# First loads in the order of the first products, and two key tiles for the keys that are formed early for block 3

## The chip, the cores and the metric

The kernel runs on one core of a Trainium2 chip. The metric is device time in microseconds (us) for one execution; lower is better. Times before are from three runs; in addition one execution was recorded by the hardware profiler, and all traced times below come from that one. The engines are TensorE (PE, with its weight loads shown as PEld), VectorE (DVE), ScalarE (ACT), GpSimd (POOL) and SyncE (SP). In this kernel SP does no arithmetic: it issues the DMAs, one after another, in program order.

## The reference

Two sequences (b = 0 and 1) of 256 tokens with 256 features each run through a "Perceiver" of four blocks. Each block has a cross-attention on a context of 4096 rows of 256 features, a self-attention and a feed-forward. Every part is added to its input after a layer norm without weights:

```
x = x + xattn_n(layernorm(x), ctx[, mask]);  x = x + attn_n(layernorm(x));  x = x + ffn_n(layernorm(x))
```

Three parts matter here.

- Block 0, cross-attention: one head, q = x Wq + bq, k = ctx Wk + bk, v = ctx Wv + bv, softmax with a mask on the context rows.
- Block 0, self-attention: normalized again, q and k are exp(-t*t/2) of a projection, out = q (k^T v) / (q sum(k) + 1e-6) over 16 heads; then a scaled norm, a 512-wide product with GELU, and a product back. Block 0, feed-forward: `h = silu(x w1) * (x w2)` (1024 wide), `gelu(h h1)`, `gelu(h h2)`, `h w3`; h1 and h2 are 1024 by 1024.
- Block 3, cross-attention: 16 heads of 16 features on the same context, `k = ctx k_w + k_b`, `v = ctx v_w + v_b`. Its keys and values depend on the context alone, so nothing in blocks 0 to 2 has to be done before them.

## The kernel before

**Arithmetic.** Nearly every product of 32-bit numbers is made of three products: each operand is a pair of tiles, a rounded high part `h` and the rest `l`, and `mm3` issues h·h, h·l and l·h. `split` (L394 to L407) makes the pair from a raw tile: ACT casts the high part (L404, or L401 with a bias), and DVE (L407, or L402 with a bias) or POOL (L406) subtracts for the low part. A weight is loaded raw (tile `wr`, L340), then split into `w`.

**Two lanes.** Tiles of the left lane have names that begin with `a`, those of the right lane with `x` (so `xkvk` is tile `kvk` of lane x, `awr` a raw weight of lane a). Each lane has its own PSUM tags and pools. The program is written lane after lane; a scheduler of the tile framework, which has its own model of the engines, sets the order in which each engine issues the instructions of both lanes. All DMAs are issued by SP in that order. An instruction waits for what it reads, and a write to a tile waits until the readers of its earlier contents are done; with `bufs=1` a tile name has one buffer, with `bufs=2` two that alternate.

**The start.** `run` (L1814 on) loads the unit matrix `eye`, both halves of x (L1818), `cols` (columns of biases and scales, L1820), the constants `first` and `unmask`, computes `w1h` and `w12` from `cols` on DVE (L1827, L1828), and calls `gone_keys` (L1305 to L1307: it loads the key mask, inverts it on DVE and writes it to device memory as `gone_d`; the attention reads it back, L716). Then `x_queries(0, xb[0])` loads x0.wq and x0.wk, normalizes x[0] (`layernorm`: L426, L427 and L432 on DVE, the power on POOL L417, the scaling L441 on DVE), transposes it on PE (L449), splits it (`axnT`) and makes the queries. After it `prep_alone(xp, 0, FIRST)` loads the weights x3.wk and x3.wv and forms the block-3 keys and values of units 0 and 1 of sequence 0.

**Keys and values of block 3.** The context of a sequence has 8 units of 512 rows. For each unit `prep_alone` (L847) loads two raw tiles of the transposed context (L859), splits each (`kx`; ACT high, POOL low) and calls `prep` (L865). `prep` does, for each half m of the features: 12 matmuls into PSUM, then ACT writes the high part and DVE the low part of tile `kvk`, and SP writes both to device memory (L876, `akh_d` and `akl_d` in the trace, 256 KB each). Then POOL sets ones in the value tile `kvv` (L878, one buffer), 24 more matmuls follow, DVE (L384) and ACT (L386) copy two results each into `kvv`, and SP writes it (L886, `av_d`, 544 KB). The same names serve three calls that stand in `run` as

```
FIRST, BEFORE, BEHIND = (0, 2), (2, 4), (4, 6)
...
self.prep_alone(xp, 0, range(*self.BEFORE), 2)
...
xb[1] = self.l0_attn(x, 1, xb[1], w0)
...
xb[0] = self.l0_ffn(0, xb[0], fp)
xq[0] = self.x_queries(1, xb[0])
self.prep_alone(xp, 0, range(*self.BEHIND), 2)
```

FIRST works in the large pool "x" and has two buffers for `kvk`. BEFORE and BEHIND, units 2 to 5, work in a smaller pool "x0", and `prep_alone` passes on `bufs=1 if bufs else 2`: one buffer for `kvk` there. The m = 1 half of a unit can then be written only after the DMAs that read the m = 0 half have landed.

**The stage with units 2 to 5.** Lane a runs `l0_ffn(0, ...)` (L984): w1 and w2 (with a tanh on ACT and `ag`, `au` on DVE), the 16 weight pieces of h1 and h2, each loaded, split and used for 24 matmuls (the GELU is L1010 on ACT), and w3 with its scaling on DVE (L1017) and the sum on POOL (L1018). Lane x runs units 2 and 3, then `l0_attn(1, ...)` (L904), then units 4 and 5. When `l0_ffn` is through, lane a goes on with `x_queries(1, xb[0])`: layer norm, transposes, casts, products. The next stage opens pool "x" again; its first context loads wait until those products are done.

**Pool "x0".** `l0_attn` gets its tiles from the same memory: `xr` and the scaled, transposed `xrTs`, `sq`, `kx`, `vx`, `kv`, `u`. `rmsnorm_t` (L891) takes a tile of the tag `xr`, too; `transposed` (L452) names the scaled tile after its tag, `xrT` + "s".

## Time and profile before

| what | value |
|---|---|
| median of three runs | 1523.76 us (1521.26 to 1531.1) |
| the profiled execution's own time | 1522.72 us |
| its span | 1520.9 us, so 1.82 us lie around it |
| mean granted TensorE clock | 0.942 |
| PE busy | 1354.9 us, 89% of the span |
| DVE, ACT, POOL busy | 1111.6, 890.3, 519.4 us |
| moved by DMA | 212.00 MB, mean 139 GB/s |

The span is the recorded stretch from the first to the last instruction. A row of the trace's timeline reads: start, duration, engine, source line, operation, output tile, input tiles, number, and in brackets the idle time of the engine just before, with what ended it. So `[3.63 <-DMA av_d<-xkvv]` says that the engine stood for 3.63 us until the DMA that reads tile `kvv` had landed. In a table of windows each row is a stretch of the span: its borders, its length, and for each engine the busy time and the number of instructions, then the granted clock, the share of the DMA engines in use and GB/s.

### The profile page before, as it was taken

To read this page: it belongs to the slowest core of one execution; us is meant where nothing else is said; L and a number is where in the kernel's file an instruction comes from. 1 tells how busy PE (TensorE), PEld (TensorE's weight loads), DVE (VectorE), ACT (ScalarE), POOL (GpSimd) and SP (SyncE) were. 2 spreads that over 40 slices of the span, in tenths; PEclk is the share of its full clock that TensorE was granted. 3 is DMA by queue.
4 is the path that set the end of the run, shared out by engine and by line. 5 is a ranking of instruction groups with operands and counts; after the bars stand their busy time and mean duration, and the time that the engine had idled before them with its cause. 6 is when DMAs were issued, how large, how long until landed. Compare 5 with 4: busy or idle time off the path is not lost.

```text
span 1520.9 us, 29330 instructions
## 1 busy us (share of the span) xinstructions
PE 1354.9 (89%) x11278; PEld 1109.5 (73%) x11278; DVE 1111.6 (73%) x1879; ACT 890.3 (59%) x1668; POOL 519.4 (34%) x389
## 2 busy tenths in 40 slices
PE   6998787968999998998998777899999999988698
PEld 6898787968998998998898435555555554874598
DVE  6999854437567878885578598799999961566675
ACT  6676555538776655764663302788888888233243
POOL 6755343236355544664335403000000000531130
PEclk9999999989999999999999859899999999996699
DMA  8754164556465657455632542343333311401262
GB/s 291 245 153 127 42 187 136 175 178 208 150 192 171 178 176 211 147 155 178 182 108 90 186 161 90 112 123 105 123 119 106 116 53 52 144 1 32 82 219 73
DMA packets 125143, 212.00 MB, mean 139 GB/s; under 512 B 12840, under 2 KB 89240, under 8 KB 121480
## 3 DMA queue, kind: packets, MB, share of 16 engines
q1 hardware_dynamic: 125004, 210.13, 44.9%
q8 instruction: 89, 1.46, 0.4%
q14 instruction: 50, 0.41, 0.1%
HBM read 181.32 MB, written 28.61 MB: 138 GB/s over the span
## 4 chain that ended last, share of the span: by engine, by line
PE 40%; DVE 24%; DMA 5%; ACT 4%; POOL 3%; issue 3%; SPq 1%; DVEq 0%; ACTq 0%; POOLq 0%
DVE xpm L1377 14%; PE amm L413 8%; PE xmm L413 6%; PE xacc L581 4%; PE xs L413 4%; PE xpr L413 4%; DMA awr<-in_w 3%; PE xf L1375 2%; PE amm L1398 2%; PE amm L1771 1%; PE xmm L785 1%; POOL aw L406 1%; ACT aw L404 1%; PE amm L581 1%; DVE aw L407 1%
## 5 line engine op out<-in xcount | busy, mean ns | idle before, releaser
L1377 DVE TENSOR_REDUCE xpm<-xf 128x2 f32<-128x1024 f32 x256 | 310.6, 1233 | 10.1 <-PE xf L1375 8.8
L1399 ACT ACTIVATE xp<-amm 128x512 f32<-128x512 f32 x342 | 194.6, 595 | 33.5 <-PE amm L1398 16.7
L406 POOL TENSOR_TENSOR aw<-awr,aw 128x1024 fp32r<-128x1024 f32 (+1 forms) x53 | 126.3, 2384 | 160.2 <-ACT aw L404 128.1
L404 ACT CAST aw<-awr 128x1024 fp32r<-128x1024 f32 (+1 forms) x112 | 114.0, 1020 | 102.7 <-DMA awr<-in_w 53.2
L413 PE MATMUL xmm<-xvx,xpT 128*128 128x256 f32 x1152 | 167.2, 291 | 5.0 <-DVE xpT L788 2.2
L413 PE MATMUL xs<-xkx,xqkT 128*128 128x256 f32 x1152 | 162.0, 285 | 1.5 <-POOL xkx L735 0.7
L735 POOL TENSOR_TENSOR xvx<-xraw,xvx 128x512 fp32r<-128x512 f32 x96 | 132.6, 1397 | 87.4 <-ACT xvx L733 82.9
L581 PE MATMUL xacc<-xp,xv 128*17 128x256 f32 x2048 | 161.0, 387 | 0.9 <-DVE xot L599 0.9
L1375 PE MATMUL xf<-xk,xq 64*128 64x512 f32 x512 | 135.3, 526 | 21.8 <-DVE xpm L1377 14.2
L413 PEld LDWEIGHTS xmm<-xvx,xpT 128*128 128x128 f32 x1152 | 147.9, 193 | 8.4 <-issue 3.7
L413 PEld LDWEIGHTS xs<-xkx,xqkT 128*128 128x128 f32 x1152 | 147.5, 191 | 3.4 <-POOL xkx L735 0.9
L1375 PEld LDWEIGHTS xf<-xk,xq 64*128 64x128 f32 x512 | 51.2, 196 | 126.3 <-issue 79.9
L407 DVE TENSOR_TENSOR aw<-awr,aw 128x1024 fp32r<-128x1024 f32 (+1 forms) x59 | 83.3, 1415 | 64.9 <-ACT aw L404 63.0
L1398 PE MATMUL amm<-xq,xk 64*128 64x256 f32 x684 | 112.4, 294 | 2.7 <-DVE aqT L402 2.6
L1422 POOL TENSOR_TENSOR ax<-ax,ax 128x128 f32<-128x128 f32 x8 | 3.7, 458 | 324.2 <-DVE ax L611 324.2
L1399 ACT ACTIVATE xp<-xs 128x512 f32<-128x512 f32 x170 | 101.2, 595 | 16.5 <-PE amm L1398 11.8
L413 PE MATMUL amm<-ah,aw 128*128 128x256 f32 x768 | 102.2, 290 | 9.3 <-ACT au L1010 4.9
L413 PE MATMUL amm<-axnT,aw 128*128 128x256 f32 x636 | 99.0, 313 | 10.9 <-ACT axnT L404 4.8
L1398 PEld LDWEIGHTS amm<-xq,xk 64*128 64x128 f32 x684 | 95.4, 187 | 17.2 <-issue 12.8
L413 PEld LDWEIGHTS amm<-ah,aw 128*128 128x128 f32 x768 | 96.9, 195 | 12.3 <-ACT au L1010 5.5
L413 PEld LDWEIGHTS amm<-axnT,aw 128*128 128x128 f32 x636 | 90.9, 216 | 18.5 <-ACT axnT L404 6.5
L735 POOL TENSOR_TENSOR xkx<-xraw,xkx 128x512 fp32r<-128x512 f32 x48 | 73.0, 1521 | 85.0 <-ACT xkx L733 84.8
(593 smaller groups left out, 2835.5 us busy)
## 6 DMA issues: line engine op xcount, KB each, us to landing
awr<-in_w SPq DMA_DIRECT2D x105, 512.0 KB
xraw<-in_ctxT SPq DMA_DIRECT2D x108, 256.0 KB
xraw<-in_ctx SPq DMA_DIRECT2D x96, 256.0 KB
xk<-akh_d SPq DMA_DIRECT2D x64, 256.0 KB
av_d<-xkvv SPq DMA_DIRECT2D x16, 544.0 KB
xv<-av_d SPq DMA_DIRECT2D x32, 272.0 KB
akh_d<-xkvk SPq DMA_DIRECT2D x32, 256.0 KB
akl_d<-xkvk SPq DMA_DIRECT2D x32, 256.0 KB
```

Of the source, the lines that this page charges most:

```text
L404: nc.scalar.copy(dst.h, src)
L406: return lo.tensor_tensor(dst.l, src, dst.h.bitcast(F32), ALU.subtract)
L407: return nc.vector.tensor_sub(dst.l, src, dst.h)
L413: tie(self.nc.tensor.matmul(out, lhsT=x, rhs=y, start=start and i == 0, stop=stop and i == 2))
L581: inst = self.nc.tensor.matmul(acc[STRIP * j : STRIP * j + v(j).shape[1], :S], lhsT=v(j), rhs=p[:, j, :], start=start, stop=stop)
L735: nc.gpsimd.tensor_tensor(x.l, r, x.h.bitcast(F32), ALU.subtract)
L785: tie(nc.tensor.transpose(pst[:, t * P : (t + 1) * P], p[:, t * P : (t + 1) * P], self.eye))
L1375: tie(nc.tensor.matmul(both[:, h * 512 : (h + 1) * 512], lhsT=q4[rows, j, t * P : (t + 1) * P], rhs=k4[rows, j, :], start=True, stop=True))
L1377: nc.vector.tensor_reduce(at, both.rearrange("p (h n) -> p h n", h=2), axis=AX.X, op=ALU.max)
L1398: tie(nc.tensor.matmul(ps[h][:, j, :], lhsT=ks[c][rows, a + j, s * P : (s + 1) * P], rhs=q4[rows, a + j, :], start=True, stop=True))
L1399: exps = [nc.scalar.activation(p[:, h, a : a + 2, :], ps[h], AF.Exp, scale=0.25) for h in range(2)]
L1771: nc.tensor.matmul(ps[:, f, :], lhsT=w1[half][:, c, f * P : (f + 1) * P], rhs=buf[:, c, e * cap : (e + 1) * cap], start=c == 0, stop=c == 1)
```

## The change

1. **Start.** Only x[0] is asked for ahead of the first weights. The load of `cols` is given to `x_queries` as `behind` and asked for behind the loads of x0.wq and x0.wk. `gone_keys()`, the load of x[1], the constants `first` and `unmask`, and the DVE computations of `w1h` and `w12` stand behind `prep_alone(xp, 0, FIRST)` in the program.
2. **Keys.** `prep_alone` no longer passes a number of buffers to `prep`, so `kvk` has two buffers in pool "x0" as well. `kvv` keeps one.
3. **Room.** In `l0_attn` the second result of the layer norm takes tag `kv` in place of `xr`, the scaled transposed tiles take tag `kx` in place of `xrTs`, and the tile of `rmsnorm_t` takes tag `u` with two buffers. The tags `kv`, `kx` and `u` belonged to tiles of `l0_attn` that are written later.

No arithmetic is added or removed.

```diff
-    def transposed(self, x, pool, tag, n=2, scale=None, bias=None, plain=None, bufs=1):
+    def transposed(self, x, pool, tag, n=2, scale=None, bias=None, plain=None, bufs=1, scaled=None):
...
-                u = self.t(pool, [P, 2, S], tag + "s", bufs=1)
+                u = self.t(pool, [P, 2, S], scaled or tag + "s", bufs=1)
...
-    def x_queries(self, n, x):
+    def x_queries(self, n, x, behind=lambda: None):
...
         wq, wk = k.weights(f"{pre}.wq", f"{pre}.wk")
+        behind()
...
-            self.prep(xp, b, u, kx, *w3, bufs=1 if bufs else 2)
+            self.prep(xp, b, u, kx, *w3)
...
     def rmsnorm_t(self, k, x, ap, scale):
-        xr = k.t(ap, [P, 2, D], "xr")
+        xr = k.t(ap, [P, 2, D], "u", bufs=2)
...
-        return k.transposed(xr, ap, "xrT", scale=scale)
+        return k.transposed(xr, ap, "xrT", scale=scale, scaled="kx")
...
     def l0_attn(self, k, b, x, wp=None):
-            xn, xr = k.layernorm(x, ap, second=("xr", D / self.RMS**2, 0.0))
+            xn, xr = k.layernorm(x, ap, second=("kv", D / self.RMS**2, 0.0))
...
-            xrT = k.transposed(xr, ap, "xrT", scale="a0.s1")
+            xrT = k.transposed(xr, ap, "xrT", scale="a0.s1", scaled="kx")
...
     def run(self):
-        for b in range(B):
-            nc.sync.dma_start(xb[b], self.ins["x"][b * S : (b + 1) * S, :].rearrange("(t p) d -> p t d", p=P))
+        load_x = lambda b: nc.sync.dma_start(xb[b], self.ins["x"][b * S : (b + 1) * S, :].rearrange("(t p) d -> p t d", p=P))
+        load_x(0)
         self.cols = a.t(self.fix, [P, NCOL], "cols")
-        nc.sync.dma_start(self.cols, self.ins["cols"])
-        self.first = a.const(self.fix, "first")
-        self.unmask = a.const(self.fix, "unmask").to_broadcast([P, S])
+        self.w1h, self.w12 = a.t(self.fix, [P, 8], "w1h"), a.t(self.fix, [P, 8], "w12")
...
-        self.w1h, self.w12 = a.t(self.fix, [P, 8], "w1h"), a.t(self.fix, [P, 8], "w12")
-        nc.vector.tensor_scalar(self.w1h, a.col("f0.w1", 0, 8), 0.5, None, ALU.mult)
-        nc.vector.tensor_mul(self.w12, self.w1h, a.col("f0.w2", 0, 8))
-        self.gone_d = self.gone_keys()
...
-                        xq = {0: self.x_queries(0, xb[0])}
+                        xq = {0: self.x_queries(0, xb[0], lambda: nc.sync.dma_start(self.cols, self.ins["cols"]))}
                         self.prep_alone(xp, 0, range(*self.FIRST))
+                        self.gone_d = self.gone_keys()
+                        load_x(1)
+                        self.first = a.const(self.fix, "first")
+                        self.unmask = a.const(self.fix, "unmask").to_broadcast([P, S])
+                        nc.vector.tensor_scalar(self.w1h, a.col("f0.w1", 0, 8), 0.5, None, ALU.mult)
+                        nc.vector.tensor_mul(self.w12, self.w1h, a.col("f0.w2", 0, 8))
                         xb[0] = self.xattn(xp, 0, 0, xb[0], xq[0])
```

## The prediction

> **What bounds the kernel now.** The page's busy table comes first: PE is busy 89% of the span at a mean granted clock of 0.942, and the chain that ended last is PE 40%, DVE 24%, DMA 5%. So only a stage in which PE stands idle can give time to this change. The table of windows shows three (borders, length, busy time and instructions of PE, PEld, DVE, ACT, POOL; clock; DMA share; GB/s):
>
> ```profile
> 7.70:48.00 40.30, 33.43 (x237) 31.23 (x238) 30.83 (x42) 28.34 (x51) 32.04 (x20) 1.00 0.94 320
> ...
> 187.00:312.70 125.70, 109.05 (x816) 104.91 (x817) 61.16 (x96) 63.90 (x106) 51.26 (x34) 0.95 0.56 170
> 312.70:337.30 24.60, 13.60 (x80) 12.06 (x80) 9.38 (x25) 7.16 (x13) 6.45 (x6) 0.73 0.50 141
> ```
>
> The start is bound by transfers: a DMA share of 0.94. The stage from 187 us, in which units 2, 3 and 4 are formed beside l0_ffn(0) and l0_attn(1), leaves PE idle 125.70 - 109.05 = 16.65 us. The seam, from the end of l0_ffn's last product (312.7, called T0 below) to the next stage's loads, leaves 11.00 us at a clock of 0.73.
>
> Who ends the idle time in the stage is told by its waits (total, times, longest):
>
> ```profile
> ACT aw L404 <- DMA awr<-in_w: 20.8, 11, 3.9
> ...
> PE xpr L413 <- DVE xkvk L402: 6.8, 2, 3.5
> ...
> PE amm L413 <- ACT au L1010: 4.7, 2, 3.9
> ...
> ACT xkvk L401 <- DMA akl_d<-xkvk: 3.7, 2, 3.0
> ```
>
> The last line is the single kvk tile. The first is its competitor: lane a stands for weights.
>
> The timeline shows the waits for both kinds of tile, in the stage and in the seam:
>
> ```profile
> 221.09 0.42 DVE L384 COPY xkvv<-xmm 128x256 f32<-128x256 f32 x1 [3.63 <-DMA av_d<-xkvv]
> ...
> 223.35 1.69 PE L413 MATMUL xpr<-xw,xkx 128*128 128x256 f32 x12 [3.46 <-DVE xkvk L402]
> ...
> 229.36 0.69 ACT L401 ACTIVATE xkvk<-xmm,acols 128x512 fp32r<-128x512 f32 x1 [3.04 <-DMA akl_d<-xkvk]
> ...
> 323.75 0.69 ACT L401 ACTIVATE xkvk<-xmm,acols 128x512 fp32r<-128x512 f32 x1 [4.68 <-DMA akl_d<-xkvk]
> ...
> 325.60 1.22 PE L449 MATMUL amm<-ac_eye,axn 128*128 128x128 f32 x4 [7.45 <-DVE axn L441]
> ```
>
> PE's 3.46 us at 223.35 name kvk, but kvk stood behind the value copies, which waited for av_d (issued at 213.01, landed at 221.09: 8.08 us). That is kvv's single tile, which stays single. At 323.75 it is kvk: akl_d was issued at 316.84 and landed 6.9 us later; DVE stood behind ACT, the layer norm's scaling (325.14) behind DVE, and PE for 7.45 us.
>
> **The start.** Before, the first weight is asked for at 4.26, behind x[1], cols, first, unmask and the key mask, and ACT casts it at 8.37. DVE does x[1]'s statistics (0.72 us and more, from 5.07) ahead of the value that POOL's power waits for. Meanwhile the DMA engines are not full:
>
> ```profile
> 2.00:3.00 1.00, 0.00 (x0) 0.00 (x0) 0.00 (x0) 0.01 (x1) 0.00 (x0) 1.00 0.77 160
> ...
> 5.00:6.00 1.00, 0.00 (x0) 0.00 (x0) 1.00 (x9) 0.00 (x0) 0.00 (x0) 1.00 0.56 52
> ```
>
> From 2 to 7 us the shares are 0.77, 0.98, 0.76, 0.56 and 0.78, so 1.15 us of transfer time is lost. After, SP issues eye, x[0], the lane-a weight, cols, the lane-x weight and four context tiles, then the key mask, x[1], first, unmask. The weight is asked for about 2.6 us earlier. POOL's low part of it (9.49 to 11.85) then follows the power, which starts 0.8 us earlier (x[1]'s statistics are gone): from about 7.2, 2.3 us earlier, and with it the four low parts of the context tiles (6.53 us from 11.81). Against this, DVE's low part of axnT (0.69 at 9.94) now stands behind that of the lane-x weight (2.06), about 1.4 later. From 7 to 24 us DMA runs at 0.9 and more, so what is regained of its time counts most: I take **-1.5**, between 1.15 and 2.3 and nearer the transfers. Ends: -3 (POOL's 2.3 and x[1]'s statistics in full), +1 (the DVE order, and the mask's round trip, now behind the weights and the context, late for the first softmax).
>
> **The stage up to T0.** No instruction is added to the arithmetic. With two tiles both halves of a unit's keys stand together on ACT and DVE, with no DMA between them. The order of the program moves, too: w1 and w2 of l0_ffn come ahead of l0_attn(1)'s exponentials and of unit 3, and the largest part of the new order is at the end: PE issued 34 matmuls of units 4 and 5 behind T0 (10 + 5 + 5 + 2 + 12 on the timeline from 312.52), and now issues 70, so 36 leave the stage. Before T0, 28 matmuls of the w3 product take 3.50 us (309.18), 0.125 each, and 36 take 4.5 us, moved into a seam with 11 us of idle PE. The key tile's stall at 229.36 left PE idle 1.44 at 231.48, which goes. Sum **-5.9**. What is late next is lane a's weight: a pair comes every 7.2 to 8.5 us on the timeline.
>
> Ends: -14.3, if all idle time goes but 3.46 at 223.35 and 3.36 at 189.39, in the end of the attention before (16.65 - 6.82 = 9.8), and the 4.5 come on top; +2.6, if nothing is won and two more ACT table loads (tanh and exponential now alternate; 1.28 us each at 0.73) stand bare. I cost them at nothing because ACT is busy 63.90 of 125.70 us. The tags kv, kx, u cost nothing either: they add one wait, POOL's sum `base` for DVE's low part of xrT, and POOL is busy 51.26 of 125.70.
>
> **The seam.** The stall of 4.68 on ACT goes, but the LN's way does not come free. POOL's memset of unit 5's kvv now stands ahead of the LN's power, and ACT's copies into it ahead of the axnT cast; both wait until unit 4's av_d has landed. On SP that av_d stands behind two weight loads, the second of which waits for a POOL low part: this load was issued at 317.97, T0 + 5.3. From there av_d takes 4.4 (issued 307.93, memset at 312.30) to 8.1 us; then memset 0.22, power 1.37, scaling 1.37, transposes 1.24. So axnT is cast at T0 + 13.9 to 17.6, where it was 326.86 - 312.68 = 14.18: -0.3 to +3.4. I take the middle, **+1.6**. PE does the 70 matmuls in this time, 70 x 0.125 = 8.75 us, so the value tile's wait hides them; without it the 36 would cost their 4.5 again.
>
> A rule weighed against the rows. The rows: akl_d took 6.9 us from issue to landing, av_d 4.4 and 8.1. The Trainium skill (DMA: Bandwidth & Descriptors, Anatomy of one DMA) gives one transfer a fixed part of about 2.0 us, mostly completion latency, and its 256 KB at 436 GB/s another 0.6; by that estimate a second tile could win 2.6 us at most where the rows lose 6.9. The rows decide, since these writes share the engines with weight loads. A second rule speaks for more: after the 7.45 us idle, 12 matmuls took 3.45 us against 1.60 at full clock. The skill (TensorE: Matmul & The Clock Gate, Part 1) puts the drop to half clock after some 3.4 us idle; a seam without such a gap would win those 1.85 us too. I leave them out, since the value tile keeps a gap.
>
> After the seam the program's order is the same but for small swaps: 0.
>
> **The sum**, on the profiled execution's own 1522.72 us (span 1520.9 and 1.82 around): -1.5 - 5.9 + 1.6 = -5.8, so **1516.9**. The median of the runs is 1.04 higher.
>
> **Rivals.**
>
> 1. *The keys held up the whole chain.* For it: 6.8 us of PE waits on kvk, and the chain of waits in the seam runs through 6.81 us of akl_d. Against: 20.8 us of ACT waits for weights. Then all of -14.3 comes, and the seam its -0.3: 1522.72 - 1.5 - 14.3 - 0.3 = 1506.6. Chance 0.13.
> 2. *The single value tile takes the keys' place* (slower). Place: unit 3's value copies on DVE and ACT, ahead of lane a's copies. SP issues unit 2's av_d behind a weight load that waits for a cast and a POOL low part (1.05 + 2.39 = 3.44). If the flight (8.08) and this lie bare, PE stands 11.52, of which 3.46 were there: +8.06, and the seam's end of +3.4: 1522.72 - 1.5 - 5.9 + 8.06 + 3.4 = 1526.8. It decides once the added value waits pass the 7.4 us won at the start and before T0. For it: 7.13 on POOL and 3.63 on DVE at 221.1. Against: av_d also landed in 4.4. Chance 0.2.
> 3. *The change gives no lead:* weights set T0 whatever the keys do. For it: the 20.8 us. Against: PE's waits on kvk. Only the start and the seam count: 1522.72 - 1.5 + 1.6 = 1522.8. Chance 0.22.
>
> **How the numbers follow.** The forecast has 0.45. The ends add up to 1522.72 - 3 - 14.3 - 0.3 = 1505.1 and 1522.72 + 1 + 2.6 + 3.4 = 1529.7; rounded out by the 1.04 between profile and median the range is 1504 to 1531 and takes in all rivals. One per cent, about what a measurement of this kernel can tell from no change, is 15.2 us: faster is below 1508.5, most of rival 1 with a little of the forecast, 0.12; slower is above 1539, only what I have not thought of, 0.05; the rest 0.83.
>
> **What would show it.** Start: first weight cast on ACT near 6, attention's steps some 1.5 earlier at 48 us. Stage: no wait of ACT's kvk for akl_d, T0 near 312.7 - 7.4 = 305.3, stalls of value copies on av_d no longer than 4. Seam: POOL's memset of kvv, not kvk, as the last wait ahead of the LN, some 26 us from T0 to the next stage's first load (now 24.6). I am wrong if a stall on av_d of 8 us or more stands bare on PE, or if l0_ffn's weights come no earlier than before.

## The result, and the profile after

The kernel became slightly **slower**: the median of 22 runs is 1530.33 us (1523.37 to 1535.76), against 1524.65 us (1514.68 to 1534.88) of 22 runs of the kernel before. The ratio is 1.0039, 95% interval 1.0021 to 1.0057, or about 5.7 us more where 5.8 us less were forecast. The recorded execution took 1535.49 us, with a span of 1533.7 us and a mean granted clock of 0.936 (0.942 before); it is among the slowest of the 22.

The table of windows for the kernel after, with the borders moved to about the same places of the program (304.10 is 1.3 us behind T0, which is 302.8 here), and then the stage behind the seam, which the prediction did not show (start:end, length, then busy time and number of instructions of PE, PEld, DVE, ACT and POOL, granted clock, DMA share, GB/s):

```profile
9.45:48.00 38.55, 31.44 (x226) 29.48 (x227) 30.55 (x41) 23.49 (x44) 27.75 (x18) 1.00 0.92 298
187.00:304.10 117.10, 103.60 (x803) 99.65 (x804) 67.93 (x96) 66.77 (x106) 51.01 (x31) 0.99 0.54 175
304.10:324.80 20.70, 15.04 (x107) 13.98 (x106) 9.50 (x26) 7.75 (x17) 8.95 (x8) 0.92 0.60 189
...
324.80:350.00 25.20, 18.59 (x125) 18.19 (x124) 18.71 (x25) 16.58 (x30) 15.59 (x11) 0.82 0.69 219
...
400.00:440.00 40.00, 33.97 (x243) 33.33 (x244) 15.83 (x26) 29.78 (x45) 13.45 (x8) 0.87 0.42 136
440.00:485.00 45.00, 41.60 (x328) 41.25 (x328) 32.71 (x67) 26.31 (x57) 22.29 (x17) 0.92 0.53 161
```

The same view of the kernel before, for that stage:

```profile
337.30:360.00 22.70, 18.95 (x153) 18.37 (x152) 20.34 (x26) 18.73 (x34) 17.61 (x10) 0.99 0.83 247
...
400.00:440.00 40.00, 37.15 (x301) 35.92 (x300) 20.81 (x37) 32.01 (x51) 17.78 (x11) 1.00 0.52 160
440.00:485.00 45.00, 43.94 (x369) 43.48 (x367) 33.85 (x74) 26.79 (x59) 22.89 (x17) 1.00 0.59 179
```

The two stages on which the prediction worked did become shorter: from 187 us to T0 115.8 us for 125.7, and 22.0 for 24.6 from T0 to the last border, with a clock of 0.92 for 0.73 in the seam. The next stage lost it again. In the 40 us from 400 to 440 PE did 243 matmuls, where the kernel before did 301 in the same time, at a clock of 0.87 for 1.00.

The waits of the kernel after in the stage up to the seam (engine, line, releaser: total, times, longest, in us):

```profile
ACT aw L404 <- DMA awr<-in_w: 16.2, 11, 3.0
...
POOL xkvv L880 <- DMA av_d<-xkvv: 8.0, 2, 6.6
...
PE amm L413 <- ACT au L1012: 4.0, 2, 2.5
...
DVE xkvv L384 <- DMA av_d<-xkvv: 2.5, 1, 2.5
```

ACT's waits for `akl_d` are gone, the value tile's wait on DVE is 2.5 us for 3.63 before, and its long one is POOL's, as before (6.6 for 7.1). ACT's waits for weights fell from 20.8 to 16.2 us.

The timeline of the kernel after: the start, the seam, the next stage's first loads with the PE stall behind them, and PE's three longest stalls of that stage (the idle time just before is in the brackets):

```profile
5.76 1.04 ACT L404 CAST aw<-awr 128x1024 fp32r<-128x1024 f32 x1 [3.75 <-DMA awr<-in_w]
...
6.88 2.36 POOL L406 TENSOR_TENSOR aw<-awr,aw 128x1024 fp32r<-128x1024 f32 x1 [1.00 <-ACT aw L404]
6.95 2.77 DVE L441 TENSOR_SCALAR axn<-ax,abn_mv,abn_rs 128x256 f32<-128x256 f32 x2
...
9.45 1.23 PE L449 MATMUL amm<-ac_eye,axn 128*128 128x128 f32 x4 [9.45 <-DVE axn L441]
...
306.39 0.38 SPq L888 DMA_DIRECT2D av_d<-xkvv  x1
...
311.70 0.21 POOL L880 MEMSET xkvv<- 128x64 f32 x1 [1.17 <-DMA av_d<-xkvv]
...
312.54 1.54 DVE L441 TENSOR_SCALAR axn<-ax,abn_mv,abn_rs 128x256 f32<-128x256 f32 x4 [1.92 <-POOL abn_rs L417]
...
323.98 0.60 ACT L398 ACTIVATE xqkT<-amm 128x512 fp32r<-128x512 f32 x1 [0.68 <-PE amm L413]
...
326.85 0.89 SPq L725 DMA_DIRECT2D xraw<-in_ctxT  x2
...
330.77 0.58 PE L413 MATMUL xs<-xkx,xqkT 128*128 128x256 f32 x1 [2.24 <-ACT xkx L735]
...
345.37 2.93 PE L413 MATMUL amm<-axnT,aw 128*128 128x256 f32 x12 [4.37 <-DVE ag L1031]
...
409.82 0.79 PE L413 MATMUL amm<-ah,aw 128*128 128x256 f32 x2 [2.87 <-ACT aw L404]
...
471.29 2.93 PE L413 MATMUL xmm<-xvx,xpT 128*128 128x256 f32 x12 [3.40 <-DVE xo L803]
```

PE's stall of 7.45 us in the seam is gone. The three stalls at the end have no counterpart in the kernel before: from the next stage's first loads to 500 us, its longest PE stall is 2.25 us.

To say where the time went in each kernel, the program is cut at five instructions that every version has: the first, second and third sum of an attention's result with its input (DVE, L842, or L844 after: S1, S2, S3), the first scaling of an `l0_ffn` product (DVE, L1017 or L1019: F), and the last write of block 1's first queries (ACT, L398: Q). F comes 0.87 us behind the point called T0 in the prediction. Each number is from one recorded execution, in us.

| kernel | to S1 | S1 to S2 | S2 to F | F to Q | Q to S3 | rest |
|---|---|---|---|---|---|---|
| before | 114.2 | 77.0 | 122.4 | 22.8 | 162.0 | 1022.6 |
| after | 116.1 | 78.5 | 109.0 | 20.3 | 179.1 | 1030.6 |
| start_only | 114.2 | 78.7 | 108.4 | 26.5 | 177.1 | 1020.6 |
| keys_only | 116.7 | 78.6 | 111.1 | 19.0 | 162.1 | 1030.0 |
| keys_old_order | 115.1 | 77.0 | 111.7 | 20.1 | 161.2 | 1029.9 |
| room_old_order | 113.8 | 76.9 | 115.6 | 24.0 | 162.4 | 1030.9 |
| late_new_order | 116.5 | 78.5 | 120.1 | 21.8 | 173.9 | 1027.6 |
| late_old_order | 117.2 | 81.3 | 108.3 | 22.0 | 166.5 | 1023.0 |

The rest does not rank with the kernels' times: the recorded executions differ in it by up to 10 us, and keys_old_order has a longer rest and a better time than before. So it is left out of what follows, and whole times are compared by medians only. The stages scatter, too: up to S1 the seven traces with the old start (back_act and best, below, among them) need between 112.6 and 116.7 us, and late_new_order and room_old_order, which have one key tile and the order of before up to Q (but for one POOL sum in the second), need 120.1 and 115.6 us from S2 to F, for 122.4 in before. Without the rest, after stands to before by +1.9 + 1.5 - 13.4 - 2.5 + 17.1 = +4.6 us, near the 5.7 of the medians. **In these two traces the gain came, and more than forecast (13.4 + 2.5); the stage from Q to S3 took it back and more.**

### The profile page after: what moved, and what is told of

It is laid out like the page before. It is cut to its first block, busy times and chain, and to the rows that moved or that the text cites. A ratio compares the mean times of both kernels' runs of the same rounds, so it can differ in the third digit from the quotient of the medians.

```text
span 1533.7 us, 29332 instructions
## 1 busy us (share of the span) xinstructions
PE 1365.5 (89%) x11278; PEld 1118.7 (73%) x11278; DVE 1119.7 (73%) x1879; ACT 900.2 (59%) x1674; POOL 520.4 (34%) x389
## 4 chain that ended last, share of the span: by engine, by line
PE 44%; DVE 24%; ACT 6%; DMA 6%; POOL 3%; issue 3%; SPq 0%; DVEq 0%; ACTq 0%; POOLq 0%
DVE xpm L1379 14%; PE amm L413 10%; PE xmm L413 7%; PE xs L413 5%; PE xacc L581 4%; PE xpr L413 4%; DMA awr<-in_w 3%; PE xf L1377 2%; PE amm L1400 2%; ACT aw L404 2%; PE amm L1773 2%; PE xmm L787 1%; POOL aw L406 1%; DMA av_d<-xkvv 1%; DVE aw L407 1%
## 5 line engine op out<-in xcount | busy, mean ns | idle before, releaser
L404 ACT CAST aw<-awr 128x1024 fp32r<-128x1024 f32 (+1 forms) x112 | 113.8, 1019 | 98.2 <-DMA awr<-in_w 48.5
L413 PE MATMUL xs<-xkx,xqkT 128*128 128x256 f32 x1152 | 165.3, 289 | 3.0 <-ACT xkx L735 2.2
L413 PEld LDWEIGHTS xs<-xkx,xqkT 128*128 128x128 f32 x1152 | 151.1, 196 | 5.0 <-ACT xkx L735 2.4
L1377 PE MATMUL xf<-xk,xq 64*128 64x512 f32 x512 | 135.8, 528 | 20.1 <-DVE xpm L1379 12.1
```

Source lines behind the costliest of these rows:

```text
L404: nc.scalar.copy(dst.h, src)
L413: tie(self.nc.tensor.matmul(out, lhsT=x, rhs=y, start=start and i == 0, stop=stop and i == 2))
L1377: tie(nc.tensor.matmul(both[:, h * 512 : (h + 1) * 512], lhsT=q4[rows, j, t * P : (t + 1) * P], rhs=k4[rows, j, :], start=True, stop=True))
```

## The experiments

All kernels below compute the whole reference. Some are **held to an order**: at the end of the program each engine's instructions are linked in a given order with dependencies that only rank them and wait for nothing, so that the scheduler cannot choose. The order is that of another kernel, or one spliced at a point. The link, the same in all of them (the list is left out):

```diff
-        Perceiver(ctx, tc, ins, out).run()
+        p = Perceiver(ctx, tc, ins, out)
+        p.run()
+        p.pin()
...
+    def pin(self):
...
+                if last is not None:
+                    self.tc.add_manual_dep(inst, last.name, order, reason="pinned")
```

The kernels of one section without another remark ran beside the same runs of the kernel before.

### Which part of the change, and is it the order?

**start_only**: part 1 of the change alone, the scheduler free.

```diff
-            self.prep(xp, b, u, kx, *w3)
+            self.prep(xp, b, u, kx, *w3, bufs=1 if bufs else 2)
...
-        xr = k.t(ap, [P, 2, D], "u", bufs=2)
+        xr = k.t(ap, [P, 2, D], "xr")
```

> The first transfers in the new order, one key tile as before. In the trace of the changed kernel the first weight is cast at 5.76 us instead of 8.37, but the two scalings of the first layer norm on DVE take 2.77 us instead of 0.72, beside POOL's low part of that weight, and PE's first transposes start at 9.45 instead of 7.68. Theory (the start loses by itself): DVE scaling near 2.8 us, first transposes near 9.4, +1 to +3.5 us in the attention from 50 to 190 us, and about +2 to +3.5 us in all, near 1527. Rival (the start gains, and what was lost up to 190 us came from the other part): -1.5 us, near 1523.

Measured: 1530.08 us against 1522.37, ratio 1.0053 (1.0029 to 1.0077).

**keys_only**: parts 2 and 3 alone, the scheduler free.

```diff
-                        xq = {0: self.x_queries(0, xb[0], lambda: nc.sync.dma_start(self.cols, self.ins["cols"]))}
+                        xq = {0: self.x_queries(0, xb[0])}
...
-                        self.gone_d = self.gone_keys()
-                        load_x(1)
...
```

> Two key tiles and the shared tags, start as before; the scheduler orders everything anew. Theory (parts add): nothing lost at 187 us, the last product of l0_ffn(0) some 13 us earlier than before (about 299.5), but the stage after it (l0_ffn(1) beside block 1's first attention) takes 14 us longer than before, since its order comes out as in the changed kernel: about -13 + 14 = +1, near 1525.5. Rival (the loss after 325 us is the start's doing through the order it brings): the gain of 9 to 13 us stays, near 1513.

Measured: 1514.73 us, ratio 0.9943 (0.9920 to 0.9966).

**keys_old_order**: keys_only, held to the order of the kernel before from end to end. POOL's sum `base` (L976) stands up to three POOL instructions later, since its tile now shares a tag.

```diff
 order of each engine
-as scheduled for keys_only
+as in the kernel before, all of it
```

> Two key tiles and the shared tags, start as before, and every engine's instructions held to the order of the kernel before; only POOL's sum for l0_attn's output stands up to three POOL instructions later, because its tile is now shared. So this shows what the tile alone brings. Theory (the tile removes waits, the order takes the gain back): no wait of ACT's key copy for a key write; the 7.45 us on PE at 325.60 shrink by the 4.68 that ACT waited, the 1.44 at 231.48 go; -5 to -7 us in all, near 1518.5. Rival (the gain of 13 us before the seam was the new order's, the tile alone brings nothing): 0 to -2, near 1523.5.

Measured: 1515.78 us, ratio 0.9940 (0.9917 to 0.9963).

**late_old_order**: the kernel after, with the order of the kernel before from block 1's queries (about 324 us) on.

```diff
 order of each engine
 up to block 1's queries: as scheduled for the kernel after
-behind them: as scheduled for the kernel after
+behind them: as in the kernel before
```

> The changed kernel, with its own order up to the queries of block 1 for sequence 0 (about 324 us), and from there on the order of the kernel before on every engine. No other edit. Theory (the order of the stage from 325 to 480 us loses what the tiles won): PE's idle of 4.37, 2.87 and 3.40 us at 345, 410 and 471 and the lower clock after them go, the lead of about 9.5 us at 325 us stays to the end: near 1515. Rival (the stage loses it whatever its order, because its transfers and weights come no earlier): about +5 as in the changed kernel, near 1530.

Measured: 1519.87 us, ratio 0.9993 (0.9972 to 1.0013).

What follows: the key tiles alone win 8.7 us (0.0057 x 1522.37) and the new start alone loses 8.1. Together they should then leave nothing, and after is 5.9 slower (0.0039 x 1524.65): the gain of the tiles is mostly not there once the start is new, though the three intervals leave that open by some 5 us. The loss is one of order and lies behind the seam: late_old_order changes nothing but ranks there, and the time falls from 1.0039 to 0.9993. The table shows the same: Q to S3 takes 161 to 162 us in keys_only and keys_old_order, 166.5 in late_old_order, 177 to 179 in start_only and after. start_only has no second key tile, and nearly the order of after in that stage (14 PE instructions stand elsewhere); keys_only has nearly that of before (48). Between before and after 147 of 1216 PE, 19 of 178 ACT, 21 of 185 DVE and 6 of 53 POOL instructions of the built order stand elsewhere from Q to S3. **The new start moved the stage behind the seam through the scheduler, 300 us further on in the program.**

What is left in late_old_order, 4.5 us over before, does not come from the order of this stage. One thing that its trace and that of after show is late first context loads of the next stage. The kernel before:

```profile
336.34 0.89 SPq L723 DMA_DIRECT2D xraw<-in_ctxT  x2
336.35 0.60 ACT L398 ACTIVATE xqkT<-amm 128x512 fp32r<-128x512 f32 x1 [1.48 <-PE amm L413]
```

There they are asked for at Q. In after they come at 326.85, 2.9 us behind Q (323.98), and PE stands 2.24 us for them at 330.77; the wait of 4.3 us that ended last on SP is for `av_d`, unit 5's value tile. In late_old_order they come 2.5 us behind Q, and PE stands 1.71 us. The loads come 1.6 to 3.0 us behind Q in all ten traces that have the order of after or of start_only ahead of Q, and at Q in the other seven. How much of the 4.5 us this makes up was not tested.

### The other way round, the tile alone, and the start

**late_new_order**: the kernel before, untouched in its code, with the order of the kernel after from about 336 us on.

```diff
 order of each engine
 up to 336 us: as in the kernel before
-behind it: as in the kernel before
+behind it: as scheduled for the kernel after
```

> The kernel before (old start, one key tile), held to its own order up to the queries of block 1 for sequence 0 (about 336 us), and from there on to the changed kernel's order on every engine. Theory (that order costs by itself): PE stalls of 3 to 4 us in the stage of l0_ffn(1) come up, the markers after it stand 10 to 17 us later than before, time near 1535 to 1540. Rival (the stage's loss needs the changed kernel's earlier start into it, since its transfers come no earlier): 0 to +3, near 1524.

Measured: 1539.16 us against 1525.72, ratio 1.0088 (1.0055 to 1.0121), from only four runs of it: 13.4 us, of which Q to S3 shows 11.9 in the table. So of the 17.1 us of after some 12 go with the order of the stage itself, and the 4.5 of late_old_order with what stands ahead of it.

**room_old_order**: keys_old_order with one key tile, so that only the tile differs between the two.

```diff
-            self.prep(xp, b, u, kx, *w3)
+            self.prep(xp, b, u, kx, *w3, bufs=1 if bufs else 2)
```

> As keys_old_order, the same order on every engine and the same shared tags, but one key tile. So the two differ in the second tile alone. Theory (the second tile brings the gain): ACT's waits for key writes are back (3.04 and 4.68 us), T0 and the time as in the kernel before, near 1523. Rival (POOL's later sum or the shared tags brought it): near 1515.8 as with two tiles.

Measured: 1523.92 us, ratio 0.9989 (0.9968 to 1.0011): holding a kernel to an order costs nothing that shows. Against 0.9940 of keys_old_order the second key tile alone is worth some 0.5%, 7.5 us; the table has it as 4.0 from S2 to F and 3.9 from F to Q. The timeline of room_old_order, with the ACT wait that the prediction had shown for before at 229.36:

```profile
228.76 0.69 ACT L469 ACTIVATE xkvk<-xmm,acols 128x512 fp32r<-128x512 f32 x1 [3.03 <-DMA akl_d<-xkvk]
```

and the same instruction in keys_old_order:

```profile
226.64 0.68 ACT L465 ACTIVATE xkvk<-xmm,acols 128x512 fp32r<-128x512 f32 x1
```

The wait of 3.03 us on ACT is gone whole, although PE's own idle time for this tile was only 1.44 us: counted from S2, the instruction comes 34.6 us on, where room_old_order has 38.1.

**low_behind_axn**: the kernel after in its own order, with one wait more: POOL's low part of the first weight (`made["Pool"][-384]`) stands behind DVE's scaling of x[0] (`made["DVE"][-1873]`).

```diff
+        self.tc.add_manual_dep(made["Pool"][-384], made["DVE"][-1873].name, landed, reason="behind")
```

> The changed kernel in its own order, with one wait more: POOL's low part of the first weight waits for the two scalings of the first layer norm on DVE. Theory (POOL's low part and DVE's scaling keep each other off, and POOL got in first): the two scalings take 0.72 us and not 2.8, nor do they wait 2.4; the first transposes start near 7.2 us and not at 9.4 to 9.9; the attention's end at 114 us (first sequence) comes some 2 us earlier than in the changed kernel, as early as in the kernel before; all in all -2 us against the changed kernel, near 1527. Rival (the scaling is late for another reason): first transposes at 9.4 or later.

Measured: 1534.93 us, ratio 1.0064 (1.0040 to 1.0088). The scaling takes 0.73 us again and the transposes start at 7.15 us instead of 9.45, but S1 still comes at 116.0 us and the time does not fall.

**best**: two key tiles, the old start, the order of before up to S1, of after up to block 1's queries, and of before behind them.

```diff
 order of each engine (code of keys_only)
-as scheduled for keys_only
+up to S1: as in before; up to block 1's queries: as in after; then as in before
```

> Old start, two key tiles; held to the order of the kernel before up to the end of the first attention (114 us), then to the changed kernel's order up to the queries of block 1, then to the old one. Theory (the changed kernel's order before the seam is better than the old one, by the 36 products moved behind it, once the start loses nothing): T0 near 300.5 instead of 303.7 with the old order throughout, all later markers about -15 to -16 against the kernel before, near 1508. Rival (with two key tiles the order before the seam makes no difference): as keys_old_order, near 1515.8.

Measured: 1520.35 us, ratio 0.9961 (0.9939 to 0.9983). It is not better than keys_old_order: S2 to F is 112.5 us for 111.7, and S1 to S2 80.2 for 77.0. The new order from S1 to Q, with its 36 matmuls moved behind T0, wins nothing once the second tile is there.

### Which swaps cost the time behind the seam?

Four kernels with the code of after; each takes back a piece of its order, or uses only a piece.

```diff
 fix_1: order from Q, about 325 us, to about 350 us
-as in after
+as in before
 fix_12: order from Q to the end of l0_ffn(1, ...), about 440 us
-as in after
+as in before
 fix_3, DVE, near 467 us
-amf<-ami (L1319), xo (L803)
+xo (L803), amf<-ami (L1319)
 new_start_old_rest: order behind S1
-as in after
+as in keys_old_order
```

> The changed kernel in its own order, but in the stretch from the queries of block 1 up to the last product of l0_ffn(1)'s second linear (about 325 to 350 us) in the old order. In that stretch the changed order puts this product of 12 matmuls ahead of 16 score products of the other lane, and PE stood 4.4 to 5.4 us for its activation (DVE, tile ag) in every kernel with the new order. Theory (three places of the new order cost, this is the first): that stall goes, those of 2.9 us (ACT, weight cast, near 410) and 3.4 us (DVE, xo, near 471) stay; from the queries to the end of the attention's first result (marker y3) 5 to 7 us less than in the changed kernel, time near 1524. Rival (the loss is the stage's, and moves on to the next place when one is mended): no gain, near 1530.

> As the run before, but old order up to the end of l0_ffn(1) (about 440 us). Theory: the stalls near 345 and 410 both go, the one of 3.4 us near 471 stays; 9 to 12 us less than in the changed kernel, near 1520. Rival: no more gain than with the first stretch alone.

> The changed kernel in its own order on every engine, with two neighbours on DVE exchanged: the attention's running sum xo (L803, 0.47 us) now ahead of the mask's conversion amf (L1319, 4.2 us beside POOL's work). Nothing else differs. Theory (three places): PE's stall of 3.40 near 471 goes, and the slower clock after it; 3.5 to 5 us less than in the changed kernel, near 1526. Rival: another wait takes its place, near 1530.

> The changed kernel (new start, two key tiles), in its own order up to the end of the first attention (114 us), from there on in the order of keys_old_order. Against keys_old_order it differs in the start alone. Theory (the new start by itself neither gains nor loses more than 1 us; it cost through the order it led the scheduler to): near 1516 to 1517, -0.5 to -0.6%. First rival (the start gains its 1.5 us once the order is mended): near 1514. Second rival (the start loses 3 to 7 us, as the markers at 191 us of some traces have it): near 1519 to 1523.

Measured, against 1523.74 us of before: fix_1 1530.12, ratio 1.0040 (1.0020 to 1.0061); fix_12 1526.09, 1.0023 (1.0004 to 1.0042); fix_3 1527.71, 1.0019 (1.0001 to 1.0036); new_start_old_rest 1517.55, 0.9958 (0.9936 to 0.9980).

fix_1 does nothing: the stall at 345.37 goes, and one of 2.85 us comes at 351.57. fix_12 brings Q to S3 from 179.1 to 167.9 us, though its ratio is only 0.0016 (2.4 us) below that of after. In fix_3 a single swap of two DVE instructions takes 4.0 us from Q to S3 (175.1). Its timeline shows them, and PE's product, without a wait (in after it stood 3.40 us):

```profile
467.20 0.48 DVE L870 SCALAR_TENSOR_TENSOR xo<-xo,xdown,xmm 128x256 f32<-128x256 f32 x1
...
467.74 4.33 DVE L1386 TENSOR_SCALAR amf<-ami 64x128 f32<-64x128 int32 x1
...
468.79 1.68 PE L480 MATMUL xmm<-xvx,xpT 128*128 128x256 f32 x12
```

`amf<-ami` turns a mask of 64 by 128 integers into numbers. It is part of the next stage's preparation, takes 4.33 us here, and in after it stands ahead of the 0.48 us for which PE waits.

new_start_old_rest has the new start and the old order behind S1: 0.42% faster than before, where the old start with the same order had 0.60%. The intervals overlap; **no gain of the new start is to be seen.**

### The table loads

ACT loads a table when it passes from the exponential of the attention to the GELU of the feed-forward or back. The groups of ACT instructions from 312 to 490 us in the kernel before (number, then total busy time and mean ns):

```profile
L774 ACT ACT_TABLE_LOAD x7 | 9.0, 1283 | 0.1
L1010 ACT ACT_TABLE_LOAD x6 | 7.7, 1283 | 0.6 <-PE amm L413 0.5
```

and in the kernel after:

```profile
L1012 ACT ACT_TABLE_LOAD x8 | 10.3, 1283 | 1.7 <-PE amm L413 1.6
L776 ACT ACT_TABLE_LOAD x7 | 9.0, 1283 | 0.1
...
L781 ACT ACT_TABLE_LOAD x2 | 2.6, 1283 | 0.0
```

17 loads for 13. The two new ones at L781 are for an exponential of one column, 0.29 us, that stands between two GELUs; each costs a second load to come back. All kernels with the new late order and no repair of it have 17 loads in this stage, all with the old one 13. The timeline of the kernel after, ahead of PE's stall at 409.82:

```profile
404.93 1.28 ACT L1012 ACT_TABLE_LOAD   x1
406.23 0.47 ACT L1012 ACTIVATE au<-amm,acols 128x256 f32<-128x256 f32 x1
406.72 1.28 ACT L781 ACT_TABLE_LOAD   x1
408.02 0.29 ACT L781 ACTIVATE xdown<-xtop,xtop 128x1 f32<-128x1 f32 x1
...
409.78 1.28 ACT L1012 ACT_TABLE_LOAD   x1
```

Three kernels test this. fix_act moves the two exponentials ahead of the GELUs, fix_act_3 does so and fix_3's swap, and back_act puts the two between the GELUs of keys_old_order.

```diff
 fix_act, fix_act_3: ACT
-au (GELU), xdown (exp), ah, ..., au (GELU)
+xdown (exp), au (GELU), ah, ..., au (GELU)
 back_act: ACT
-xdown (exp), au (GELU), ah, ..., au (GELU)
+au (GELU), xdown (exp), ah, ..., au (GELU)
```

> The changed kernel in its own order on every engine but for two instructions on ACT: the exponentials of one column (xdown, L781, 0.29 us) that stand between two GELUs of l0_ffn(1) are put one and two places earlier, behind the exponentials just ahead of these GELUs. Four of the 17 table loads of that stage go (13 in the old order). Theory (the table loads cost: with 13 of them the stage from the queries to l0_ffn(1)'s last product took 103 to 107 us in the traces, with 17 of them 111 to 117): that stretch takes 104 to 109 us instead of 116.5, PE's stall of 2.87 near 410 goes, time 8 to 11 us under the changed kernel's, near 1520. Rival (the loads only go together with the order on PE, which does the harm): 116 us as before, or at most 5.1 less (4 x 1.28).

> As the run before, and with the exchange of xo and amf on DVE too: three one-column or short instructions stand elsewhere than in the changed kernel, nothing else. Theory (these three places are the loss of the stage): queries to the attention's result (y3) 163 to 167 us instead of 179, time near 1515 to 1517, under the kernel before. Rival (much of the loss is elsewhere): over 172 us and over 1521.

> The kernel with two key tiles and the old order, but with the same two exponentials moved the other way, between the GELUs as the changed kernel has them: 17 table loads in that stage instead of 13, nothing else. Theory: the stretch from the queries to l0_ffn(1)'s last product takes 8 to 13 us more than 103.2, time near 1525. Rival (ACT has slack, since it is busy for two thirds of the stage): 0 to 3 us more, near 1517.

Measured, against 1526.56 us of before: fix_act 1532.86, ratio 1.0041 (1.0017 to 1.0066); fix_act_3 1527.41, 1.0002 (0.9978 to 1.0026); back_act 1518.89, 0.9956 (0.9935 to 0.9976).

From Q to the second F, the part with the loads, the traces give 116.5 us for after and 111.1 for fix_act, 103.2 for keys_old_order and 107.6 for back_act: 5.4 won by taking the two exponentials out, 4.4 lost by putting them in. Other traces agree: with the code of after, four kernels with 17 loads take 116.4 to 117.2 us there (after, low_behind_axn, fix_1, fix_3), and two with 13 loads 111.1 and 112.4 (fix_act, fix_act_3). The timeline of back_act has the stall that it forces:

```profile
400.24 1.28 ACT L847 ACT_TABLE_LOAD   x1
401.53 0.29 ACT L847 ACTIVATE xdown<-xtop,xtop 128x1 f32<-128x1 f32 x1
...
403.33 0.51 PE L481 MATMUL amm<-ah,aw 128*128 128x256 f32 x2 [2.35 <-ACT aw L472]
```

fix_act's time does not show its 5 us (1.0041 for 1.0039 of after, and the intervals leave room for a gain of some 4), and its recorded execution is the fastest of its ten. back_act's 0.9956 for 0.9940 would be 2.4 us, within the intervals, too. So the table loads' price is one of the traces; the medians alone do not show it. With both repairs 1.0002 (0.9978 to 1.0026) is left: 5.6 us of the 5.9 by which after was slower. Q to S3 is still 171.8 us, against 161 to 162; PE's stalls near 346 us (4.04, for `ag`) and 428 us (2.76, for ACT's `ah`) are still there. Against keys_old_order PE is busy 6.8 us more in that stage with the same 1222 matmuls (156.81 for 150.01, at a mean clock of 0.95 for 1.00), and idle 3.8 us more; which swaps cause it was not separated.

## Why the prediction was wrong, point by point

**The step that failed** is the last ahead of the sum: "After the seam the program's order is the same but for small swaps: 0." The swaps were there to be read from the built order, and were priced by their number. The stage from Q to S3 became 17.1 us longer in the trace. Its order alone, put into the kernel before, costs 11.9 us there and 13.4 us by the medians; with the old order in it, after is still 4.5 us above before there. Two swaps are seen at work in the traces: one long DVE instruction ahead of a short one for which PE waits (4.0 us), and two exponentials of 0.29 us that force four table loads (4.4 and 5.4 us). By the medians they are clear only together (1.0039 to 1.0002). The rest of the 17.1 is not divided up.

This step explains the loss, but not all of the distance to the forecast: with the old order behind the seam, after came to 0.9993 (0.9972 to 1.0013), no difference from before, where 0.9962 had been forecast. So the terms ahead of it were not right in sum either, as the next points show. The stretch from 48 to 187 us had no term at all; from S1 to S2 the ten traces with after's order there need 78.5 to 81.3 us, the seven with that of before 76.7 to 78.7. Why is not shown.

**What bounds the kernel.** Right that only stages with PE idle can give time. But the three stages that were read were those the change aimed at; that the same table can lose where PE is near full (0.93 to 0.98 busy at a clock of 1.00 from 400 to 485 us) was not asked.

**The start, -1.5.** The first weight was cast at 5.76 us, as said ("near 6"), and POOL's low part of it stood at 6.88, 2.6 us earlier. The DMA engines were fuller, too: shares of 0.58, 1.13, 0.87, 1.02 and 0.95 in the five slices from 2 to 7 us, 4.55 us of transfers for 3.85. The gain did not come: S1 is at 116.1 us for 114.2. Moved earlier, the low part meets DVE's scaling of x[0]. In after POOL was ahead by 0.07 us and the scaling took 2.77 us for 0.72. In the trace of start_only DVE was ahead:

```profile
6.77 0.73 DVE L441 TENSOR_SCALAR axn<-ax,abn_mv,abn_rs 128x256 f32<-128x256 f32 x2
...
7.35 2.36 POOL L406 TENSOR_TENSOR aw<-awr,aw 128x1024 fp32r<-128x1024 f32 x1 [1.48 <-ACT aw L404]
```

The Trainium skill (SBUF — State Buffer, SBUF: two separate sides) says that VectorE, in a 2-port mode or with two SBUF inputs, and GpSimd share a port pair as an exclusive lock: whichever starts first holds it for its whole instruction, and the other blocks. The rows agree with it, and this rule, which speaks against moving the two together, was not weighed. Yet the collision is not the whole of it: low_behind_axn took it away and S1 stayed at 116.0 us. In the seven traces with the new start where DVE was first, S1 came between 114.2 and 116.4, in the three where POOL was first between 116.1 and 117.8. With the old start it is 112.6 to 116.7 in seven traces, so that a term of 1.5 us is below what single traces can tell. The medians show no gain of the start either (new_start_old_rest). If earlier weights make the first attention earlier at all, these runs don't show it, nor what it waits for instead.

**The stage to T0, -5.9.** T0 came at 302.8 us instead of 312.7, where 305.3 had been forecast. From S2 to F the trace shows -13.4, of which part belongs neither to the tile nor to the moved order: in before PE stood 3.87 us for a GELU at 256.83, with a clock of 0.50 from 256 to 262 us, while room_old_order, with the same order on PE and one tile, stood 1.73 us and needs 115.6 us, though its median is that of before. Two terms were mis-sized. The tile's wait was taken as PE's 1.44 us; it held up ACT for 3.03, and brings 4.0 us in this stage by keys_old_order against room_old_order. The moved order was taken as 4.5 us; start_only, with one tile and as many matmuls moved behind T0, needs 108.4 us for S2 to F, but in an order of its own (217 of 753 PE instructions stand elsewhere than in after). The two don't add up: two tiles and new order give 109.0, two tiles and old order 111.7. That both fill the same idle time would fit, but was not tested. Another reason is in the trace. The two extra table loads ahead of T0 came (the program has 23 for 17, the other four behind the seam; the pair is GELU and exponential, not tanh and exponential), and they did stand bare, against their cost of nothing, in after:

```profile
229.26 1.28 ACT L1012 ACT_TABLE_LOAD   x1
...
231.08 1.22 PE L413 MATMUL amm<-ah,aw 128*128 128x256 f32 x8 [1.50 <-ACT au L1012]
231.98 1.28 ACT L934 ACT_TABLE_LOAD   x1
...
233.74 0.70 PE L940 MATMUL xs<-xvx,xkx 128*128 128x256 f32 x2 [1.45 <-ACT xkx L934]
```

start_only and keys_old_order do not have these two. That ACT is busy for half of the stage did not hide them: each stood just ahead of an instruction for which PE was waiting. The Trainium skill's sum for one DMA (DMA: Bandwidth & Descriptors, Anatomy of one DMA), which the section gives for DMAs issued from GpSimd while here SP issues them, would have capped the second tile at 2.6 us a wait; ACT waited 3.04 and 4.68, and the tile alone was worth 7.5, so the rows were rightly preferred.

**The seam, +1.6.** It became 2.5 us shorter from F to Q, and `axnT` is cast 13.1 us behind T0 for 14.18. Unit 4's `av_d` was issued 3.6 us behind T0, not 5.3, and POOL's memset waited 1.17 us for it, where a landing at up to 8.1 us after the issue had been feared; the clock stayed at 0.92. The form of the step was right: the memset, not `kvk`, was the last wait ahead of the layer norm. From T0 to the next stage's first load it took 24.1 us, where 26 were forecast. But before it was 23.7 and not 24.6 (the first load is at 336.34, and the border stood at 337.3), so by the prediction's own mark the seam won nothing: what Q gained, the first loads lost on the wait for unit 5's `av_d`, which had no place in the sum. The second tile helps from F to Q: start_only took 26.5 us, after 20.3.

**The rivals.** None was it as priced. The value tile (rival 2, 1526.8 us, nearest to the time) shows, but not as +8.06 us on PE in the stage: there DVE's copy waited 2.50 us for `av_d` at 225.65, and PE 1.29 us behind it at 227.08, for 3.46 before. It shows in the seam, where the first loads wait for it (2.24 us of PE at 330.77). That weights alone set T0 (rival 3) is refuted by room_old_order and keys_old_order. Slower than before had been thought of only as a wait in the two stages that were changed.

**A version that beats both** is the change without its first part: keys_only at 0.9943 (0.9920 to 0.9966).

## What to carry to other kernels

Where a scheduler sets the order, an edit at the start is an edit of the whole program: compare the built order of every stage, and look in it for what order alone makes dear, such as the number of table loads and a long instruction ahead of a short one on the way to PE, before writing 0. Price a tile's wait by the engine that it holds up in order, not only by the idle time of PE beside it. A mean share of busy time does not say that two table loads are hidden: look at what stands behind each. Measure each part of a change alone: here one was worth -0.6% and the other +0.5%. And read a stage's length from several traces: with nearly the same order, the stage to F took 115.6 to 122.4 us.

## What the runs showed of the hardware

**A stall of PE can cost up to 1.7 times its length.** Two-microsecond windows of the kernel after, around the stall of 3.40 us at 471.29 (columns as above):

```profile
468.00:470.00 2.00, 0.00 (x0) 0.00 (x0) 2.00 (x1) 0.52 (x1) 2.00 (x3) 1.00 0.00 0
...
472.00:474.00 2.00, 2.00 (x11) 2.00 (x11) 0.99 (x4) 1.01 (x3) 0.00 (x0) 0.50 0.79 270
474.00:476.00 2.00, 2.00 (x12) 2.00 (x11) 0.48 (x1) 0.00 (x0) 0.21 (x1) 0.50 0.34 99
476.00:478.00 2.00, 2.00 (x14) 2.00 (x14) 0.90 (x2) 0.00 (x0) 0.00 (x0) 0.68 0.69 193
478.00:480.00 2.00, 2.00 (x20) 2.00 (x19) 0.75 (x2) 1.47 (x3) 0.00 (x0) 1.00 0.93 329
```

From 472 to 478 us PE did 37 matmuls where at full clock it does some 20 in 2 us: about 2.3 us lost on top of the stall, by an estimate from these counts. The same followed shorter stalls: 2.87 us at 409.82 (clock 0.50 to 0.53 from 410 to 416 us), and 2.24 us at 330.77 (0.52 from 332 to 334). It does not follow each: behind 3.46 us at 223.35 in the kernel before the clock stayed at 1.00 up to 229 us, and 2.25 us at 359.72 there passed without it. The Trainium skill (TensorE: Matmul & The Clock Gate, Part 1) gives an idle window of about 3.4 us for the drop; here 2.24 us were enough, and 3.46 us once were not. Behind the same wait in late_new_order, which has the code of before and its order up to there (3.47 us at 227.50), it did fall, to 0.50. So the same stall can cost different amounts in two executions.

**A change of table costs 1.3 us, not more.** In the rows from 404.93 on, GELU, load and exponential follow each other within 0.02 us of the load's 1.28. The Trainium skill (ScalarE: Activation LUTs, What ACT_TABLE_LOAD costs) adds a drain of about 1.4 us to each switch; none is seen. What made the switch dear is its place, between a weight's cast and the product that waits for it.
